# Unused expert tiles moved into a branch, with p7's additions, the last bias and the squared sums rearranged, in a two-layer fp32 kernel

## The chip, the cores and the metric

The kernel runs on one core of a Trainium2 chip. The metric is the device time of one execution in microseconds. A core has five engines that run beside each other, each in the order of its own instruction stream: TensorE (PE in the profile; PEld is its weight load), VectorE (DVE), ScalarE (ACT), GpSimd (POOL) and SyncE (SP, which here issues DMAs). They wait for each other through semaphores.

## What is computed

The input is 2048 tokens of 512 numbers. The first layer adds three things to them: a gated linear attention of 32 heads of 128, a shared expert, and a mixture of 16 small experts of which each token takes two. A second, smaller layer follows (attention of one head and a low-rank mixture). All of it is fp32. Cut to the part that the change is about:

```python
logits = xt @ router_w + router_b
scores = softmax(logits) + router_bias
keep   = the 2 best of 4 groups of experts, by each group's best score
idx    = the 2 best experts among the kept           # for each of 2048 tokens
for e in range(16):
    h = silu(xt @ ew1[e] + eb1[e]) * (xt @ ew2[e] + eb2[e])
    y += gate[:, e] * (h @ ew3[e] + eb3[e])
y += shared expert, with its own last bias sb3

attn = causal linear attention with decay, heads of 128
out  = (sigmoid(x @ gate_w.T) * norm_w * attn * rsqrt(mean(attn**2) + eps)) @ out_w.T
```

## The kernel before

**Opening** (to about 120 us). Tokens are normalized, transposed and routed. Each token's two choices become slots of a list that is sorted by expert; each expert's part of the list is rounded up to whole tiles of 128 slots. The worst routing needs `NMT` = 47 tiles, so the kernel has 47. `ends` holds, in its last column, the number of tiles that the routing really uses; `whose` says whose token stands in a slot, `own_` and `rows_` which expert owns a tile. A tile that no expert uses is worked on as if it were the last expert's, and nobody reads its rows of `yd`.

**Attention.** The long middle part is 4 chunks of 512 tokens (i) by 8 groups of four heads (g): 32 *units*, numbered i * 8 + g. The projection of a unit is a product of matrices cut into halves, done with 7 half-size products instead of 8, two levels deep: 7 *outer products* p1, p2, p6, p5, p3, p7, p4 (`ORDER`), each of 7 inner products of four 128 x 128 matmuls (`product`, L730 to L738; L735 is the matmul). In the first chunk some outer products are done plainly. `Outer.result` (L1106) takes an inner sum out of PSUM: into r and from there into a (POOL, DVE) or straight into b, c or d. Four quarters a, b, c, d of the unit's result become whole after p2, p3, p7 and p4, and each then goes through `Quarter` (L825): silu and gate on ACT, scores, attention, squared sums, and the output projection (`Unit.project`, L944), which sums over all units of a chunk in `acc`. When a chunk's last unit is done, `done`, `combine` and `finish` (L1030, L634, L640) turn `acc` into the attention's part of the layer's result.

**The order of the work** is written out by hand. After each inner product `slot()` (L755) is called; `later(n, f)` puts a piece of other work n slots ahead, and `slot()` runs at most one or two of those that are due, where some named pieces don't count. On ACT and POOL the instructions keep the order of the source (`manual_schedule`); on TensorE, DVE and SP a scheduler may move them. DVE's order in the built program is thus not always that of the source.

**Expert tiles** run inside the units of chunks 1 to 3. `expert(j)` (L1187) starts tile j; `Expert` (L765) gathers its 128 tokens and the expert's weights by two indirect DMAs on POOL (L772, L777), turns the tokens with 4 transposes (L786), gathers the bias (L792), multiplies (8 matmuls, L804; one of 512 columns, L816) and stores 256 KB to `yd` (L822). On TensorE an fp32 matmul is two instructions, a transpose is one. From the unit where g is 0 of each chunk, two tiles are started, else three in early units (`EARLY`) and two later:

```python
for e in range(3 if g > 0 and i * NG + g < FROM + EARLY else 2):
    if todo:
        later((24 if g == 0 else 1) + 16 * e, partial(expert, todo.pop(0)))
```

**Buffers.** r and the tiles' result ye share three buffers of the tag "sum" (2 KB a partition each). The last bias of the shared expert, `sb3`, takes one of them at each chunk's end: `load_sum` (L1023) loads it, and `last_bias` (L651) adds it at once with four additions on POOL. Weights w rotate in three buffers, the output projection's weights wo in seven. `attend` (L864) squares 512 columns on ACT and adds all 512 to `sums` on POOL; at a chunk's end the two halves are added. Of `p7` the result r is added into a on POOL and into c on DVE, in the same step.

## Time and profile before

| what | us |
|---|---|
| median of 3 runs | 2780.84 (2780.56 to 2783.33) |
| the profiled execution's own time | 2780.53 |
| its span, first to last instruction | 2778.5 |
| granted TensorE clock, mean | 0.997 of full |
| TensorE busy / weight loads | 2733.5 / 2522.7 |
| DVE / ACT / POOL busy | 1627.6 / 947.2 / 1649.8 |

Names in the profile are those of the program without buffer numbers: `ps_a`, `ps_b`, `ps_e`, `ps_sc`, `ps_o` are PSUM banks, `xt` the tokens' sums, `w` the weights. L100 is the line of a helper that adds or subtracts (L101 in the changed kernel), so additions are told apart by their tiles, not by their line; `c<-c,r` may add into a, b, c or d, which all bear the name c. In a row of a stretch, "busy (x)" is busy time and number of instructions. A bracket at the end of a timeline's line is the engine's idle time just before it and what ended it. Matmuls overlap each other, so the durations of single matmuls don't add up to time; distances between starts do.

The chunks show in the profile: the first (units 0 to 7) runs to about 701, the second to 1305, the third to 1896, the fourth to 2464, and the second layer fills the rest.

### The profile page before, as it was taken

The numbers are of one execution on the slowest core, as the hardware profiler recorded it, in microseconds if no ns is written. First come the engines' busy times: TensorE is split into PE (matmuls) and PEld (weight loads), VectorE is DVE, ScalarE is ACT, GpSimd is POOL, SyncE is SP. The second block draws the span as 40 slices with busy tenths as digits, with TensorE's granted clock in tenths as the row PEclk, the third lists the DMA queues.
The fourth block names the chain that finished last, engine by engine and source line by source line (L and its number), as shares of the span: only waits on it lengthen the run. The fifth ranks groups of instructions, "written<-read, shape, count | busy, mean of one in ns | idle before, by whom it ended". The sixth has DMA issues, their size and how long they took to land.

```text
span 2778.5 us, 49222 instructions
## 1 busy us (share of the span) xinstructions
PE 2733.5 (98%) x19492; PEld 2522.7 (91%) x19492; DVE 1627.6 (59%) x2733; ACT 947.2 (34%) x1683; POOL 1649.8 (59%) x1422
## 2 busy tenths in 40 slices
PE   9999999999999999999999999999999999999999
PEld 5699999999999999999999999999999999987877
DVE  7656777776545555555545555555555555667663
ACT  5232222222433333333343333334433333432221
POOL 6477777776566666665855555556555567553210
PEclk9999999999999999999999999999999999999999
DMA  7898898888977777777877777787877788653211
GB/s 296 310 339 335 311 334 325 337 315 330 352 274 261 288 272 277 265 280 288 304 250 253 253 257 251 264 288 268 281 255 255 270 298 295 218 215 124 78 63 63
DMA packets 155445, 735.87 MB, mean 265 GB/s; under 512 B 18768, under 2 KB 25296, under 8 KB 112848
## 3 DMA queue, kind: packets, MB, share of 16 engines
q1 hardware_dynamic: 137056, 661.89, 64.8%
q0 software_dynamic: 17872, 70.32, 7.7%
q8 instruction: 154, 2.52, 0.4%
q14 instruction: 75, 0.61, 0.1%
q10 hardware_dynamic: 288, 0.52, 0.1%
HBM read 587.84 MB, written 144.04 MB: 263 GB/s over the span
## 4 chain that ended last, share of the span: by engine, by line
PE 86%; DVE 6%; POOL 3%; issue 3%; DMA 2%; ACT 0%; SPq 0%; DVEq 0%; POOLq 0%; ACTq 0%
PE ps_a L735 25%; PE ps_e L735 13%; PE ps_sc L948 10%; PE ps_b L735 7%; PE ps_sc L968 4%; PE ps_o L869 4%; PE ps_sc L857 3%; PE ps_sc L804 3%; PE ps_o L870 2%; PE ps_sc L858 2%; PE ps_a L1676 2%; PE ps_sc L816 1%; DVE w L100 1%; PE ps_a L1579 1%; PE ps_a L359 1%
## 5 line engine op out<-in xcount | busy, mean ns | idle before, releaser
L735 PE MATMUL ps_a<-xt,w 128*128 128x128 f32 x5376 | 751.3, 276 | 16.3 <-DVE r L100 7.6
L735 PEld LDWEIGHTS ps_a<-xt,w 128*128 128x128 f32 x5376 | 686.7, 192 | 46.0 <-issue 14.1
L100 POOL TENSOR_TENSOR c<-c 128x512 f32<-128x512 f32 x240 | 305.2, 1286 | 265.7 <-DVE c L100 263.1
L1103 ACT COPY cp<-ps_a 128x512 f32<-128x512 f32 x384 | 224.0, 584 | 659.9 <-PE ps_a L735 636.9
L100 POOL TENSOR_TENSOR c<-c,r 128x512 f32<-128x512 f32 x264 | 345.8, 1332 | 167.1 <-DVE r L100 166.6
L735 PE MATMUL ps_e<-xt,w 128*128 128x128 f32 x2688 | 374.5, 275 | 0.6 <-DVE r L100 0.3
L735 PEld LDWEIGHTS ps_e<-xt,w 128*128 128x128 f32 x2688 | 341.4, 192 | 6.7 <-issue 2.9
L735 PE MATMUL ps_a<-w,xt 128*128 128x128 f32 x1792 | 346.8, 275 | 0.0
L100 POOL TENSOR_TENSOR w<-w 128x512 f32<-128x512 f32 x224 | 297.7, 1337 | 80.5 <-DVE w L100 32.9
L100 POOL TENSOR_TENSOR sums<-sums,sq 128x512 f32<-128x512 f32 x120 | 155.8, 1298 | 277.4 <-ACT sq L884 276.8
L948 PE MATMUL ps_sc<-wo,gT 128*128 128x256 f32 x1288 | 304.9, 380 | 2.8 <-POOL gT L100 2.8
L735 PEld LDWEIGHTS ps_a<-w,xt 128*128 128x128 f32 x1792 | 272.4, 192 | 0.0
L948 PEld LDWEIGHTS ps_sc<-wo,gT 128*128 128x128 f32 x1288 | 232.9, 190 | 30.9 <-POOL gT L100 3.1
L100 DVE TENSOR_TENSOR acc<-ps_sc,acc 128x512 f32<-128x512 f32 x208 | 142.7, 689 | 195.2 <-PE ps_sc L948 150.6
L891 DVE SCALAR_TENSOR_TENSOR gT<-ps_o,nw,c 128x256 f32<-128x256 f32 x256 | 112.0, 479 | 216.1 <-ACT sq L884 206.0
L735 PE MATMUL ps_b<-xt,w 128*128 128x128 f32 x1536 | 214.8, 276 | 6.5 <-issue 3.7
L100 DVE TENSOR_TENSOR c<-ps_a,c 128x512 f32<-128x512 f32 x216 | 146.8, 687 | 120.7 <-PE ps_a L735 115.4
L735 PEld LDWEIGHTS ps_b<-xt,w 128*128 128x128 f32 x1536 | 195.1, 193 | 9.0 <-issue 5.7
L832 ACT ACTIVATE c<-c 128x512 f32<-128x512 f32 x256 | 150.3, 628 | 146.0 <-DVE c L100 127.9
L884 ACT ACTIVATE sq<-ps_o 128x512 f32<-128x512 f32 x120 | 71.7, 597 | 358.1 <-PE ps_o L870 352.7
L100 DVE TENSOR_TENSOR s<-ps_sc,decay 128x384 f32<-128x384 f32 x256 | 139.7, 553 | 79.9 <-PE ps_sc L858 77.2
L735 PE MATMUL ps_e<-w,xt 128*128 128x128 f32 x896 | 173.5, 275 | 0.0
(297 smaller groups left out, 4723.3 us busy)
## 6 DMA issues: line engine op xcount, KB each, us to landing
w<-in_w_att_dram SPq DMA_DIRECT2D x56, 1024.0 KB
w<-in_w_att_dram SPq DMA_DIRECT2D x72, 768.0 KB
st<-in_w_att_dram SPq DMA_DIRECT2D x32, 1024.0 KB
wo<-in_w_out_dram SPq DMA_DIRECT2D x113, 256.0 KB
decay<-dec SPq DMA_DIRECT2D x64, 384.0 KB
w<-ws0p SPq DMA_DIRECT2D x12, 1792.0 KB
w<-ws1p SPq DMA_DIRECT2D x12, 1792.0 KB
w<-ws2p SPq DMA_DIRECT2D x12, 1792.0 KB
```

What stands on the lines that cost most here:

```text
L100: (eng or nc.vector).tensor_tensor(o, a, b, op)
L735: mm(bank[:, bass.ts(ty, P)], a, b, start=(first and ty == 0), stop=True, skip_group_check=True,)
L804: mm(pu[:, bass.ts(n, P)], w12[:, n, c, :], self.xeT[:, c, :], start=(c == 0), stop=(c == NC - 1),)
L832: nc.scalar.activation(qk, qk, AF.Silu)
L857: mm(p[:, 0:S], self.c[:, 2 * hh, P : 2 * P], q, start=True, stop=True)
L858: mm(p[:, S : S + P], self.c[:, 2 * hh + 1, P : 2 * P], q[:, 1, :], start=True, stop=True,)
L869: mm(po[:, bass.ts(hh, S)], v[:, 0, :], self.s[:, hh, 0:S], start=True, stop=False)
L884: nc.scalar.activation(sq, po, AF.Square)
L891: nc.vector.scalar_tensor_tensor(gT[:, h, :].rearrange("p (t n) -> p t n", t=2), po[:, bass.ts(h, S)].rearrange("p (t n) -> p t n", t=2), ...
L948: mm(py[:, bass.ts(t, S)], self.O[p][:, hh, bass.ts(t, P)], self.wo[p][:, hh, :], start=(t == 0 and hh == 0), stop=(hh == 1), skip_group_c ...
L968: mm(py[:, bass.ts(h, S)], gT[:, hh, bass.ts(t, P)], self.wo[pair, h][:, hh, :], start=(h == 0 and hh == 0), stop=(hh == 1), skip_group_ch ...
L1103: nc.scalar.copy(c, bank)
```

## The change

Five things are changed together; the diff follows.

1. **A branch.** Only tiles 0 to 35 (`USUAL`) are run in the units. The other 11 stand, one behind the other, in `beyond()`, under a condition on the number of used tiles, which the opening copies into `used`. It is called once, before p2 of unit 27 (the unit where i is 3 and g is 3). Tiles are started as three each in units 9 to 12 and two each in units 13 to 15, 17 to 23, 25 and 26, and none where g is 0. The rows of `yd` that a passed-by tile would have written are filled with a copy of tokens by 11 DMAs from DRAM to DRAM, one a unit (units 8 to 18).
2. **p7's additions.** r is now added into c on POOL, at once, and into a on DVE; the additions into a are collected and written out after the third result, and again after the fourth.
3. **The last bias** is loaded into a buffer of the tag "wo", and its four additions on POOL become pieces of their own, 10, 13, 16 and 19 slots later; the load comes 1 slot after the quarter becomes whole instead of 5.
4. **Squared sums.** `sums` holds 256 columns instead of 512; the two halves of a square are added to it one after the other, and the addition at the chunk's end goes.
5. **Buffers and times.** r and ye get four buffers instead of three, and the second part of the slots' table is read 10 slots earlier (`take_table` at 30 for 40).

```diff
@@ -38,6 +38,7 @@
 
 NMT = (NT * TOP + E * (P - 1)) // P
 NSLOT = NMT * P
+USUAL = 36
 READ = 32
 WROW = 2 * NC * INTER + C + 2
 K, TOPK, RANK, SCALING = 64, 16, 16, 2.0
@@ -549,6 +550,8 @@
     own = disp.tile([P, NMT], FP, name="own")
     nc.vector.tensor_reduce(own, owner, AX.X, ALU.add)
     nc.vector.tensor_scalar(own_, own, float(E - 1), None, ALU.min)
+    used = const.tile([P, 1], I32, name="used")
+    nc.vector.tensor_copy(used, ends[:, 0, E - 1 : E])
     nc.vector.tensor_scalar(own, own, float(E - 1), float(P), ALU.min, ALU.mult)
     nc.vector.tensor_scalar(rows_, own, part, None, ALU.add)
 
@@ -759,7 +762,7 @@
             while pieces and pieces[0][0] <= now[0] and n < (2 if len(pieces) > 12 else 1):
                 f = pieces.pop(0)[2]
                 f()
-                n += getattr(f, "func", f).__name__ not in ("silu", "bias", "gate", "read_table", "take_table", "scatter", "load_sum", "sums1", "sums2", "sums3", "sums4", "settle0", "settle1", "out_sum", "combine", "finish", "store")
+                n += getattr(f, "func", f).__name__ not in ("bias_sum", "silu", "bias", "gate", "fill_tile", "read_table", "take_table", "scatter", "load_sum", "sums1", "sums2", "sums3", "sums4", "settle0", "settle1", "out_sum", "combine", "finish", "store")
 
 
         class Expert:
@@ -817,7 +820,7 @@
                     py, self.he, self.we[:, 2 * NC * INTER : 2 * NC * INTER + C],
                     start=True, stop=True,
                 )
-                ye = attn.tile([P, C], FP, tag="sum", name="ye", bufs=3)
+                ye = attn.tile([P, C], FP, tag="sum", name="ye", bufs=4)
                 add(ye, py, self.xe)
                 nc.sync.dma_start(out=yd[bass.ts(self.j, P), :], in_=ye)
 
@@ -840,7 +843,7 @@
 
             def begin(self):
                 if self.u.g == NG - 1 and (self.pair, self.b) == (1, 0):
-                    later(5, self.u.load_sum)
+                    later(1, self.u.load_sum)
                 later(2, partial(self.silu, 0))
                 later(3, partial(self.silu, 1))
                 later(4, self.gate)
@@ -875,16 +878,15 @@
                     return
                 u = self.u
                 if u.i not in sums_:
-                    sums_[u.i] = attn.tile([P, 2, CH], FP, tag="sums", name="sums")
+                    sums_[u.i] = attn.tile([P, 2, S], FP, tag="sums", name="sums")
                 sums = sums_[u.i][:, self.b, :]
+                sq = attn.tile([P, CH], FP, tag="sq" if u.i else "cp", name="sq", bufs=1 if u.i else 5)
+                nc.scalar.activation(sq, po, AF.Square)
                 if u.g == 0 and self.pair == 0:
-                    nc.scalar.activation(sums, po, AF.Square)
+                    add(sums, sq[:, 0:S], sq[:, S:], nc.gpsimd)
                 else:
-                    sq = attn.tile([P, CH], FP, tag="sq" if u.i else "cp", name="sq", bufs=1 if u.i else 5)
-                    nc.scalar.activation(sq, po, AF.Square)
-                    add(sums, sums, sq, nc.gpsimd)
-                if u.g == NG - 1 and self.pair == 1:
-                    add(sums[:, 0:S], sums[:, 0:S], sums[:, S:], nc.gpsimd)
+                    for h in range(2):
+                        add(sums, sums, sq[:, bass.ts(h, S)], nc.gpsimd)
                 gT = u.gated()
                 for h in range(2):
                     n = u.g * HG + self.pair * 2 + h
@@ -1025,7 +1027,14 @@
                 if self.i + 1 < NCH:
                     self.r = spare8()
                     nc.sync.dma_start(out=self.r, in_=xr[self.i])
-                    last_bias(self.r, attn.tile([P, C], FP, tag="sum", name="sb3", bufs=3))
+                    b3_t = attn.tile([P, C], FP, tag="wo", name="sb3", bufs=7)
+                    nc.sync.dma_start(out=b3_t, in_=b3[E : E + 1].to_broadcast([P, C]))
+
+                    def bias_sum(t):
+                        add(self.r[:, t, :], self.r[:, t, :], b3_t, nc.gpsimd)
+
+                    for t in range(TPC):
+                        later(10 + 3 * t, partial(bias_sum, t))
 
             def done(self):
                 if self.g < NG - 1:
@@ -1066,7 +1075,7 @@
 
             def __init__(self, unit, p):
                 self.u, self.p = unit, p
-                self.steps = []
+                self.steps, self.added = [], []
                 self.following = None
                 self.w = weights(unit.i, unit.g, p, self.steps)
                 if unit.g == 0:
@@ -1127,15 +1136,21 @@
                         c_ = u.tile("c")[:, q]
                         add(c_, bank, c_)
                 else:
-                    r = attn.tile([P, 512], FP, tag="sum", name="r", bufs=3)
+                    r = attn.tile([P, 512], FP, tag="sum", name="r", bufs=4)
                     if c is None:
                         nc.scalar.copy(r, bank)
                     else:
                         add(r, bank, c)
-                    add(a, a, r, pool)
-                    if p == "p7":
+                    if p != "p7":
+                        add(a, a, r, pool)
+                    else:
                         c_ = u.tile("c")[:, q]
-                        add(c_, c_, r)
+                        add(c_, c_, r, pool)
+
+                        self.added.append(partial(add, a, a, r))
+                        if (i, j) in ((1, 1), (0, 1)):
+                            while self.added:
+                                self.added.pop(0)()
                 whole = dict(p2=("b", 0, 0), p3=("d", 0, 1), p7=("c", 1, 1), p4=("a", 1, 0)).get(p)
                 if whole and (i, j) == (0, 1):
                     Quarter(u, whole[1], whole[2], u.tile(whole[0])).begin()
@@ -1173,8 +1188,8 @@
                 self.result(0, 1, self.a, None)
 
         FROM = NG
-        EARLY = 8
-        todo = list(range(NMT))
+        EARLY = 5
+        todo = list(range(USUAL))
         plan = [(i, g, p) for i in range(NCH) for g in range(NG) for p in ORDER]
         units = []
 
@@ -1190,6 +1205,21 @@
             later(12, e.bias)
             later(14, e.up)
             later(19, e.down)
+
+        def fill_tile(j):
+
+            nc.sync.dma_start(out=yd[bass.ts(j, P), :], in_=x[0:P, :])
+
+        def beyond():
+
+            n_used = nc.values_load(used[0:1, 0:1], min_val=0, max_val=NMT)
+            with tc.If(n_used > USUAL):
+                for j in range(USUAL, NMT):
+                    e = Expert(j)
+                    e.turn()
+                    e.bias()
+                    e.up()
+                    e.down()
 
         def scatter(t, n):
 
@@ -1221,7 +1251,7 @@
                 if n == 0:
                     read_table(1)
 
-            later(40, take_table)
+            later(30, take_table)
 
         def low_sums(n):
 
@@ -1325,9 +1355,11 @@
             if k == 0:
                 u.load_decay()
                 if i * NG + g >= FROM:
-                    for e in range(3 if g > 0 and i * NG + g < FROM + EARLY else 2):
+                    for e in range(0 if g == 0 else 3 if i * NG + g < FROM + EARLY else 2):
                         if todo:
-                            later((24 if g == 0 else 1) + 16 * e, partial(expert, todo.pop(0)))
+                            later(1 + 16 * e, partial(expert, todo.pop(0)))
+                if FROM <= i * NG + g < FROM + NMT - USUAL:
+                    later(30, partial(fill_tile, USUAL + i * NG + g - FROM))
                 if i == 0:
                     for e in range(max(5 * g - 3, 0), 5 * g + 2 if g < NG - 1 else 0):
                         later(10 * (e - 5 * g) + 35, partial(scatter, e // TOP, e % TOP))
@@ -1339,6 +1371,9 @@
                     wrapped_up()
             if k == 2:
                 u.load_decay()
+            if (i, g, k) == (NCH - 1, NG - 5, 1):
+                assert not todo
+                beyond()
             u.load_out(k)
             last = outers[n - 1] if n and sevenfold(n - 1) else None
             if not sevenfold(n):
```

## The prediction, written before the result was known

> **What bounds the kernel now.** I read the page's busy rows and its chain first. (Times in us unless marked; "tile" is one expert tile of 128 slots, "unit" one group of four heads of one 512-token chunk.)

> ```profile
> PE 2733.5 (98%) x19492; PEld 2522.7 (91%) x19492; DVE 1627.6 (59%) x2733; ACT 947.2 (34%) x1683; POOL 1649.8 (59%) x1422
> PE 86%; DVE 6%; POOL 3%; issue 3%; DMA 2%; ACT 0%; SPq 0%; DVEq 0%; POOLq 0%; ACTq 0%
> ```

> TensorE is busy nearly all the time and holds 86% of the chain that ended last: what leaves TensorE's stream shortens the run, what leaves DVE or POOL does so only where TensorE waits for it. So I looked next for what one tile costs TensorE. The table of stretches gives it: three stretches, each exactly one unit long (from a mark to the same mark a unit later), with three tiles, two tiles and none.

> ```profile
> core 0: us, PE busy (x) PEld busy (x) DVE busy (x) ACT busy (x) POOL busy (x), PEclk, DMA share, GB/s
> 1077.20:1152.99 75.79, 75.79 (x580) 71.96 (x579) 40.86 (x62) 27.51 (x52) 49.45 (x41) 1.00 0.75 271
> 1449.20:1522.38 73.18, 72.77 (x557) 69.36 (x557) 39.81 (x60) 27.48 (x50) 40.80 (x34) 1.00 0.72 255
> 2183.91:2250.93 67.02, 66.61 (x513) 64.15 (x513) 36.07 (x54) 26.55 (x48) 43.76 (x32) 1.00 0.74 261
> ```

> The second and third differ by 44 matmuls, two tiles of 22 (4 transposes, 16 halves of the up products, 2 of the down product), and by 6.16: a tile costs 3.08 of wall time. Three tiles cost 75.79 - 67.02 = 8.77, as the third fills a wait of 0.4 that the other two units show (busy 0.41 under the span). Last I read TensorE's own waits, the only other time to be won (columns: total, times, longest):

> ```profile
> PE ps_a L735 <- DVE r L100: 7.6, 16, 1.3
> PE ps_a L735 <- ACT cp L1103: 5.2, 3, 1.8
> PE ps_sc L948 <- POOL gT L100: 2.8, 2, 1.6
> ```

> **Tiles.** 47 run now, whatever the routing. Counting the reference's routing of its own inputs, five experts get 1859, 140, 46, 3 and 2048 choices: 15 + 2 + 1 + 1 + 16 = 35 used tiles, under 36, so the branch is passed by and 11 tiles of TensorE work go. With f(1) = 3.08, f(2) = 6.16, f(3) = 8.77 a unit: units 8 to 27 hold now 2 units with one tile, 9 with two, 9 with three (140.5); then 12 with two and 4 with three (109.0). **-31.5**; by 11 x 3.08 it would be -33.9, my lower end. What else a tile costs, three indirect DMAs on POOL (1.03, 1.00 and 1.07 each) and work on ACT and DVE, lies beside TensorE.

> **Fourth buffer for r and ye.** Three of the 16 waits for DVE r (1.32 at 773.68, 0.49 at 1381.59, 0.48 at 1969.95) stand in the first p4 after a chunk change, where the eviction waited for POOL to release one of three buffers. A fourth removes that: **-2.3** (0 if POOL is then late anyway).

> **p7's additions.** The remaining 13 waits are this pattern, on DVE in the unit at 2250:

> ```profile
> 2247.08 0.69 DVE L100 TENSOR_TENSOR r<-ps_e,cp 128x512 f32<-128x512 f32 x1 [1.19 <-PE ps_e L735]
> 2247.88 1.80 DVE L100 TENSOR_TENSOR c<-c,r 128x512 f32<-128x512 f32 x1
> 2249.60 0.68 DVE L100 TENSOR_TENSOR r<-ps_b,cp 128x512 f32<-128x512 f32 x1
> 2250.20 0.68 DVE L100 TENSOR_TENSOR r<-ps_a,cp 128x512 f32<-128x512 f32 x1
> ```

> A 1.80 addition stands between the first eviction and the two that free PSUM, and p3 of the same product waits 0.41 for the last. The diff defers that addition in the source until after the third eviction. But DVE's order is the scheduler's, and in the built program the row after the first r is again an addition of r (now into a), then two r, then the rest: the order of before, 4 additions on DVE and 4 on POOL as before, sharing time as before. I take **0**. Bounds: -9.9 (0.58 from when p3's first matmul was due, 2250.35, to its start at 2250.93, in the 17 units that will have two tiles or none and no chunk change) if the wait does go; no loss, since a was last written by POOL two outer products earlier.

> **Bias by pieces.** At a chunk's end POOL now sits in front of a load:

> ```profile
> 1322.60 4.96 POOL L100 TENSOR_TENSOR spare<-spare,sb 128x512 f32<-128x512 f32 x4 [11.43 <-DMA sb<-in_b_dram]
> ```

> Behind it are queued sums and gT, and TensorE waits 1.65 (1330.87) and 1.10 (2335.51) for gT. Ten slots later the load has landed, and the additions come one by one: **-2.8** (0 if a single 1.33 addition still meets gT). The bias now rotates in wo's seven buffers; SP is in order, so a later wo load could slip; the longest such wait today is 11.1, and loads lie 1.5 outer products ahead: 0.

> **Chunk changes.** Two ACT cp waits (1.67 and 1.68) follow from ACT standing behind a copy into acc that waits for DVE to finish the old chunk. Without tiles in the first unit POOL loses three DMA issues (3.1) ahead of that finish. Between 0 and -3.4 I take half: **-1.7**.

> **Squares.** Two additions of 256 columns for one of 512:

> ```profile
> L100 POOL TENSOR_TENSOR sums<-sums,sq 128x512 f32<-128x512 f32 x120 | 155.8, 1298 | 277.4 <-ACT sq L884 276.8
> L100 POOL TENSOR_TENSOR sums<-sums 128x256 f32<-128x256 f32 x8 | 5.8, 726 | 0.6
> ```

> 2 x 0.726 - 1.298 = 0.15 a quarter, 24 in all with the eight first squares (8 x 1.45) and without the eight last sums: POOL's, who loses 34 with the tiles. 0; were POOL's gT on the path each time, 92 x 0.15 = +14. The 11 fills of unused rows, one copy of 256 KB each, replace tile transfers of over 1.5 MB each in the queue: 0 (one landing, 6.7, if one load were held up). The copy of the count in the opening is one small DVE instruction (nearest row 0.16): 0.

> **The branch.** New, once, in unit 27. Every engine reads the count, compares and jumps; TensorE passes over some 500 instructions, then waits for its own last matmul; SP waits for all its loads, POOL for its gathers. Behind TensorE's instruction everything is queued. No row shows a jump. The nearest is an engine's instructions arriving by DMA, and an awaited small DMA from issue to landing (those that fill or read xw):

> ```profile
> q8 instruction: 154, 2.52, 0.4%
> ```

> ```profile
> DMA to landing us min/median/max: 3.4/6.7/12.3
> ```

> 154 packets of 16 KB, 0.4% x 16 x 2778.5 / 154 = 1.15 each: TensorE's code comes in pages, and 500 instructions of its 39,000 (2 x 19492) are two of them. Bounds: 0.3 (a matmul's own end) and two landings of 12.3, 24.6; not below, as the branch removes nothing. I take one median landing, **+6.7**. SP's stop is hidden: in a ring of three a load of weights is issued about 1.5 outer products (1.5 x 67.02 / 7 = 14) before its use.

> [...] The granted clock is 1.00 in all three stretches, and no wait of TensorE in the trace is over 2.6. [...]

> **Sum**: -31.5 - 2.3 - 0 - 2.8 - 1.7 + 6.7 = -31.6. From the profiled execution's own 2780.53 (span 2778.5 and 2.0 around it; the median of the runs is 2780.84): **2749**.

> **Rivals.**
> - *The addition moves and the branch is cheap.* For: the same addition takes 0.68 where POOL is quiet (at 2391.55), so if POOL's into c starts later than its addition into a does now, the 1.80 shrinks and r is free in time. Against: the built order, and POOL starts on the same r. 2749 - 9.9 - 3.3 (a landing of 3.4) = 2736.
> - *The branch empties all engines*: two landings, 24.6, as in and out of the jump both miss; against: the exit lies next to the code it enters. 2749 + 17.9 = 2767.
> - *The branch is not passed by* (slower). Place: unit 27, price: 11 tiles in series, TensorE idle between. One tile's chain by rows: two gathers 2.03, landing 6.7, transposes 0.60, copy 0.68, up 1.95, silu 0.37, product 0.35, down 1.02, sum 0.69 = 14.4; 158 for 11, 79 if two buffers hide half. 2749 + 79 to 158 = 2828 to 2907. It decides from the 37th used tile on; my count is 35.
> - *Nothing gained*: a branch of over 33 eats all, 2775 to 2786; no row is that long.

> **How the numbers follow.** Forecast, 2741 to 2757: 0.62 (branch 3.4 to 12.3, the small waits gone or not). First rival, 2731 to 2741: 0.16. Second, 2757 to 2775: 0.15. Not passed by: 0.04. Nothing gained: 0.03. About 0.2% (5.6) can be told from no change. Faster 0.62 + 0.16 + 0.15 = 0.93, within 0.03, slower 0.04. 2733 to 2764 holds all of the forecast, most of the first rival and over half of the second: 0.84.

> **What would show it.** Units with equal tiles still 67.02 and 73.18; 36 down products (72 halves); one gap on TensorE in unit 27 of 3 to 12; no POOL wait for the bias load; p7's wait of 0.41 still there. I am wrong if units change by more than 0.6, if the gap is over 12.3, or if down products number 94.

## The result, and the profile after

The changed kernel takes 2757.95 us (median of 4 runs, 2754.57 to 2759.92) against 2780.70 for the kernel before beside it: a ratio of 0.9910, with a 95% interval of 0.9899 to 0.9922. It is faster by 22.8, where 31.6 was forecast. The profiled execution took 2759.92, with a span of 2758.2 (before: 2780.53 and 2778.5), at a mean granted clock of 0.994 (before 0.997).

The page of the changed kernel begins with the busy rows:

```profile
PE 2704.0 (98%) x19250; PEld 2499.6 (91%) x19250; DVE 1597.3 (58%) x2701; ACT 943.9 (34%) x1672; POOL 1652.5 (60%) x1509
```

TensorE has 242 matmuls fewer, 11 tiles of 22: the branch is passed by. POOL has 87 instructions more and is as busy as before, though it lost the gathers of 11 tiles. Next the table of stretches, again one unit each: two tiles, no tile, and the unit of the branch (columns as in the table shown before).

```profile
1438.30:1510.80 72.50, 72.50 (x558) 69.32 (x557) 38.85 (x60) 27.32 (x50) 42.03 (x38) 1.00 0.71 257
2161.85:2228.75 66.90, 66.45 (x514) 64.03 (x512) 35.57 (x54) 27.06 (x48) 43.90 (x36) 1.00 0.71 254
2089.80:2161.85 72.05, 68.29 (x515) 65.35 (x514) 35.45 (x54) 26.62 (x47) 35.87 (x32) 0.98 0.68 238
```

In the first row the span and TensorE's busy time are the same, 72.50: the wait of 0.41 is gone, and the unit is 0.68 shorter than the 73.18 of before. The third row is the branch's unit: TensorE is busy 3.76 less than the span, and the clock is 0.98 of full. TensorE's waits tell the other side:

```profile
PE ps_a L738 <- ACT cp L1112: 11.8, 6, 2.6
PE ps_o L872 <- DVE s L101: 6.2, 6, 2.6
...
PE ps_sc L950 <- PEq L1216: 3.8, 1, 3.8
...
PE ps_sc L950 <- POOL gT L101: 1.4, 1, 1.4
...
PE ps_a L738 <- DVE r L101: 0.4, 1, 0.4
```

The 16 waits for DVE's r (7.6) are gone but for one of 0.4. In their place the waits for ACT's cp went from 5.2 to 11.8, those for DVE's s from 1.3 to 6.2, and the branch (L1216) added one of 3.8.

**Where the time went.** I cut the profiled execution, from its first matmul to its last, at the first matmul of every unit and took from each unit's length what its matmuls take at the mean spacing in a unit of the changed kernel in which nothing is waited for (unit 19: 0.1115 a matmul of 128 columns, 0.2164 of 256, 0.4305 of 512; a tile 3.09; other widths, in the opening and the second layer, at their means there). What is left over is waiting and half clock (stretches in which the granted clock was 0.5), here called loss.

| part | before | after | change |
|---|---|---|---|
| undisturbed matmuls | | | -34.0 |
| loss in units 17 to 23, 25, 26 | 7.6 | 0.0 | -7.6 |
| loss in units 9 to 13 and 28 to 31 | 6.6 | 4.2 | -2.4 |
| loss in units 14 and 15 | 0.4 | 4.1 | +3.7 |
| loss in unit 8 | 0.2 | 5.0 | +4.8 |
| loss in units 16 and 24 (first of a chunk) | 6.1 | 9.5 | +3.5 |
| loss in unit 27 (branch) | 0.7 | 5.7 | +5.0 |
| loss before unit 8 | 34.4 | 38.1 | +3.7 |
| loss in the second layer | 12.3 | 14.5 | +2.2 |
| sum | | | -21.1 |

So the work fell by somewhat more than forecast, p7's wait went against the forecast, and the six rows with a plus gave 23 back.

### The profile page after: what moved, and what is told of

It reads as the page before. It is cut to its first block, busy times and chain, and to the rows that moved or that the text cites. A ratio compares the mean times of both kernels' runs of the same rounds, so it can differ in the third digit from the quotient of the medians.

```text
span 2758.2 us, 48688 instructions
## 1 busy us (share of the span) xinstructions
PE 2704.0 (98%) x19250; PEld 2499.6 (91%) x19250; DVE 1597.3 (58%) x2701; ACT 943.9 (34%) x1672; POOL 1652.5 (60%) x1509
## 3 DMA queue, kind: packets, MB, share of 16 engines
q8 instruction: 154, 2.52, 0.4%
## 5 line engine op out<-in xcount | busy, mean ns | idle before, releaser
L738 PE MATMUL ps_a<-xt,w 128*128 128x128 f32 x5376 | 752.1, 277 | 16.6 <-ACT cp L1112 11.8
L101 POOL TENSOR_TENSOR c<-c,r 128x512 f32<-128x512 f32 x264 | 362.4, 1396 | 161.2 <-DVE r L101 157.7
L101 POOL TENSOR_TENSOR sums<-sums,sq 128x256 f32<-128x256 f32 x240 | 180.3, 751 | 307.7 <-ACT sq L884 297.9
L950 PE MATMUL ps_sc<-wo,gT 128*128 128x256 f32 x1288 | 306.9, 382 | 5.2 <-PEq L1216 3.8
L950 PEld LDWEIGHTS ps_sc<-wo,gT 128*128 128x128 f32 x1288 | 233.9, 192 | 31.6 <-issue 4.4
L884 ACT ACTIVATE sq<-ps_o 128x512 f32<-128x512 f32 x128 | 76.5, 597 | 380.2 <-PE ps_o L873 371.8
```

What stands on the lines that cost most here:

```text
L101: (eng or nc.vector).tensor_tensor(o, a, b, op)
L738: mm(bank[:, bass.ts(ty, P)], a, b, start=(first and ty == 0), stop=True, skip_group_check=True,)
L884: nc.scalar.activation(sq, po, AF.Square)
L950: mm(py[:, bass.ts(t, S)], self.O[p][:, hh, bass.ts(t, P)], self.wo[p][:, hh, :], start=(t == 0 and hh == 0), stop=(hh == 1), skip_group_c ...
```

## The experiments

Theories. **A**: p7's wait went because the exchange of engines makes POOL start its addition after DVE's, not before it. Rivals: the fourth buffer took the wait away, or the additions written later did. **B**: the branch costs what TensorE waits for the code behind the jump, and a stretch of half clock. Rival: reading the count and jumping cost it. **C**: the new waits come from the exchange, as c is now made whole by POOL. Rivals: from the tiles' new places, the squares, or the bias. All kernels were run in sets of four beside the kernel before on the same chip (its medians 2782.56, 2781.94 and 2782.60).

| run | median us | ratio to before, 95% interval |
|---|---|---|
| changed kernel | 2757.95 | 0.9910 (0.9899 to 0.9922) |
| m2_after_again | 2756.02 | 0.9902 (0.9885 to 0.9918) |
| e1_no_branch | 2748.29 | 0.9881 (0.9867 to 0.9895) |
| e2_p7_as_before | 2765.91 | 0.9943 (0.9931 to 0.9954) |
| e5_p7_defer_only | 2762.84 | 0.9927 (0.9914 to 0.9940) |
| e4_p7_pool_later | 2762.19 | 0.9926 (0.9914 to 0.9938) |
| h1_tiles_alone | 2754.52 | 0.9899 (0.9883 to 0.9914) |
| f2_squares_whole | 2753.53 | 0.9903 (0.9887 to 0.9918) |
| f3_bias_whole | 2757.70 | 0.9904 (0.9888 to 0.9920) |
| g3_both | 2756.17 | 0.9912 (0.9898 to 0.9926) |
| m1_short_branch | 2751.15 | 0.9882 (0.9866 to 0.9899) |
| k1_first_and_deferred | 2751.76 | 0.9891 (0.9875 to 0.9908) |
| k2_tile_in_first_units | 2746.95 | 0.9873 (0.9856 to 0.9889) |

Many of these differ by less than their intervals, so I read them by the lengths of units in their profiles. These agree to 0.02 between executions in the steady units (18, 28), and all kernels here but k2 and the kernel before place the tiles alike:

| unit | 8 | 14 | 15 | 16 | 18 | 24 | 27 | 28 |
|---|---|---|---|---|---|---|---|---|
| changed | 71.41 | 74.54 | 75.19 | 71.91 | 72.50 | 71.77 | 72.03 | 67.05 |
| m2, again | 71.41 | 74.56 | 75.20 | 73.17 | 72.50 | 71.79 | 72.18 | 67.05 |
| e1, no branch | 68.66 | 76.30 | 75.20 | 72.03 | 72.50 | 71.79 | 66.34 | 66.34 |
| e2, p7 as before | 73.78 | 73.18 | 73.83 | 72.12 | 73.18 | 72.60 | 73.90 | 66.99 |
| e5, later only | 72.53 | 73.31 | 73.84 | 71.79 | 73.18 | 71.78 | 73.78 | 66.99 |
| e4, POOL later | 71.41 | 73.17 | 73.83 | 72.12 | 73.18 | 72.59 | 71.97 | 66.98 |
| h1, tiles alone | 72.33 | 73.18 | 73.83 | 72.13 | 73.17 | 71.44 | 67.01 | 67.01 |
| f2, squares | 71.43 | 74.50 | 75.19 | 71.25 | 72.50 | 69.86 | 72.04 | 66.34 |
| f3, bias | 71.36 | 74.53 | 75.20 | 73.16 | 72.50 | 71.78 | 72.00 | 66.34 |
| g3 | 68.66 | 73.29 | 73.97 | 74.01 | 72.50 | 83.50 | 66.34 | 66.34 |
| m1, short branch | 71.43 | 74.53 | 75.19 | 73.17 | 72.50 | 71.77 | 67.42 | 66.34 |
| k1 | 71.44 | 73.30 | 73.94 | 72.38 | 72.50 | 71.79 | 72.10 | 66.34 |

### p7: as before, and with the engines exchanged back

e2 writes p7's additions as before:

```diff
-                    if p != "p7":
-                        add(a, a, r, pool)
-                    else:
-                        c_ = u.tile("c")[:, q]
-                        add(c_, c_, r, pool)
-                        self.added.append(partial(add, a, a, r))
...
+                    add(a, a, r, pool)
+                    if p == "p7":
+                        c_ = u.tile("c")[:, q]
+                        add(c_, c_, r)
```

> The changed kernel with p7's additions written as before: r into a on POOL and into c on DVE, at once; all else as changed, four buffers for r and ye too. Theory (who starts first): on DVE's side the order is RARRAAA in both; the wait of p3 for r went because POOL's addition, now into c, starts after DVE's instead of 30 ns ahead, so DVE's takes 0.69 instead of 1.8. Then the waits PE ps_a <- DVE r return (13 or more, 0.41 each), units with two tiles are at 73.18 again instead of 72.50, about +10; and c is whole earlier, so the waits of 1.77 at 1156 and 1231 and the 2.6 at 767 go, about -6 to -8: 2758 to 2763 in sum. Rival (the fourth buffer took the wait away): units stay at 72.50 and the new waits go, 2750 to 2752.

e5 keeps the collecting and exchanges only the engines:

```diff
-                        add(c_, c_, r, pool)
-                        self.added.append(partial(add, a, a, r))
+                        add(a, a, r, pool)
+                        self.added.append(partial(add, c_, c_, r))
```

> The changed kernel with the additions of p7 collected and written out later as in the change, but with the engines of before: a on POOL, c on DVE (collected). The orders of DVE and of POOL, by tile names, are line for line those of the changed kernel; only which of a and c an addition writes is exchanged. Theory (the engines' exchange decides who starts first): the waits PE ps_a <- DVE r return, 73.18 in the steady units with two tiles, and the new waits behind POOL's c go: 2758 to 2763, as with the additions as before. Rival (writing them later took the wait away): 72.50, and about 2750 to 2752.

Measured: 2765.91 and 2762.84, and 73.18 in the steady units of both: the wait is back, with four buffers and with the additions written later. Theory A stands and both its rivals fall. (e2's time lies 2.9 above its forecast: the wait of 2.6 in unit 8 stayed, and unit 8 got one of 0.9 for r besides.) The rows show how. In the changed kernel, DVE and then POOL in a steady unit (start, duration):

```profile
1869.73 0.69 DVE L101 TENSOR_TENSOR r<-ps_e,cp 128x512 f32<-128x512 f32 x1 [1.13 <-PE ps_e L738]
1870.52 0.69 DVE L101 TENSOR_TENSOR c<-c,r 128x512 f32<-128x512 f32 x1
1871.13 0.69 DVE L101 TENSOR_TENSOR r<-ps_b,cp 128x512 f32<-128x512 f32 x1
```

```profile
1870.56 3.01 POOL L101 TENSOR_TENSOR c<-c,r 128x512 f32<-128x512 f32 x2 [5.62 <-DVE r L101]
```

And in e5, the same unit, DVE, POOL and the matmul of p3:

```profile
1871.33 1.80 DVE L101 TENSOR_TENSOR c<-c,r 128x512 f32<-128x512 f32 x1
1873.05 0.68 DVE L101 TENSOR_TENSOR r<-ps_b,cp 128x512 f32<-128x512 f32 x1
```

```profile
1871.31 1.28 POOL L101 TENSOR_TENSOR c<-c,r 128x512 f32<-128x512 f32 x1 [5.55 <-DVE r L101]
```

```profile
1874.38 0.94 PE L738 MATMUL ps_a<-xt,w 128*128 128x128 f32 x6 [0.41 <-DVE r L101]
```

The order on DVE is the same, r, addition, r. But in e5 POOL starts 0.02 ahead and DVE's addition takes 1.80; in the changed kernel DVE starts 0.04 ahead and takes 0.69, and it is POOL's first addition that takes 1.79 instead of 1.28 (the row joins two). At this pair, in all of these kernels, whoever starts first is undisturbed, and the other ends 1.8 after that start, in both orders. A shift of 65 ns decides over 1.1 on DVE. In the built program POOL's addition into c waits for one thing more than that into a, an earlier addition into the same c by POOL itself; that this makes the 65 ns was not tested by itself.

The delay falls on one of the two alone: in e5 DVE's addition, 0.69 when it starts first, ends 0.55 after POOL's of 1.28, and in the changed kernel POOL's ends 1.14 after DVE's of 0.69. What holds the second one back, these rows don't show. The forecast let both "share" the time and did not ask who starts first.

Theory C falls in part: units 14 and 15 drop to 73.18 and 73.83 in e2 and e5, so the waits of 1.77 there are the exchange's (as is one of 1.1 early in unit 16, which e2 and e5 have not), but unit 8 keeps its wait of 2.6 for DVE's s. In unit 14 of the changed kernel, ACT shows why:

```profile
1152.72 1.15 ACT L835 ACTIVATE c<-c 128x512 f32<-128x512 f32 x2 [5.01 <-POOL c L101]
```

POOL's additions into c stand behind sums of wo in its queue; ACT waits 5.01 for c, its copies come late, and TensorE waits for them.

e4 leaves c on DVE and means to hold POOL's addition into a back by writing it later:

```diff
-                        add(c_, c_, r, pool)
-                        self.added.append(partial(add, a, a, r))
+                        add(c_, c_, r)
+                        self.added.append(partial(add, a, a, r, pool))
```

> The changed kernel with c on DVE at once, and a on POOL collected and written out after the third and the fourth result. Theory (who starts first): DVE's first addition has the path to itself, takes about 0.7, and p3 does not wait; c is whole as early as before. So units stay at 72.50 without the waits at 767, 1156 and 1231: 2757.95 less 5 to 8, 2750 to 2753. Rival A: r is held until POOL's late addition, and DVE waits for a buffer of r: 2758 or more. Rival B: POOL's late addition then meets DVE's third one, which p4 or its quarter waits for: 2755 to 2765.

Measured: 2762.19 and 73.18, neither the theory nor its rivals. POOL started 0.02 or more ahead of DVE in all units but the first with this pattern: its queue held nothing else at that point, so the addition that was written later started as early as before. Writing it later gave POOL nothing to wait for.

### The branch

e1 drops the call (`beyond()`).

> The changed kernel without the call that reads the count and branches; the 11 tiles behind the branch are left out (this routing uses 35, so nothing that is read is missing). Theory: the branch costs the gap on TensorE in unit 27 (PE ps_sc L950 <- PEq L1216, 3.8) and the half-clock stretch of 3.413 behind it (eight matmuls at twice their time, about 1.9), together 5.7: 2757.95 - 5.7 = 2752.2, unit 27 at 66.34 as unit 29. Rival A: only the gap goes and a later wait takes its place: under 3, 2755 or more. Rival B: the stop of SP (2100.1 to 2109.1) also holds back loads and costs more than the gap: over 8, under 2750.

Unit 27 is at 66.34 as expected, 5.69 less; unit 28 loses 0.7, where POOL had started first after the branch. Units 29 and 30 are as long as in the changed kernel (66.34 and 68.44), so no load that SP's stop held back shows, though the time, 2748.29, lies where that rival (B) had it. It fell by 9.7, not 6.4: unit 8 was 2.75 shorter, the part before it 3.4, and unit 14 1.8 longer, though nothing is changed there. m2 ran the changed kernel once more to see whether such parts belong to the kernel.

> The changed kernel itself once more, beside the others of this set. The excess of the first eight units (3.9 over the kernel before) and of unit 8 differs among the variants though their code is the same there. Theory: that part is not from the change but differs from one profiled execution to the next, by where the half-clock stretches fall: the first eight units vary by 1 to 4, units 9 to 31 agree with the first profile within 0.3 but for units 14 to 16, where a stretch may or may not start. Rival: it is the change's own: the first eight units and unit 8 come out the same within 0.5. The time: 2755 to 2760.

The loss before unit 8 was 35.2 instead of 38.1, and unit 16 was 1.26 longer; unit 8 was the same. Over all profiles of variants the loss before unit 8 is 33.0 to 38.1 and that of the second layer 12.8 to 14.8: differences of single executions, and two of the table's rows (+3.7, +2.2) are not shown to be the change's.

The traces say what made unit 8 shorter in e1. Near its end one pair of additions starts almost at once, POOL's and DVE's; here in the changed kernel and then in e1:

```profile
762.75 1.27 POOL L101 TENSOR_TENSOR wo<-wo 128x512 f32<-128x512 f32 x1
762.76 3.47 DVE L101 TENSOR_TENSOR c<-c,r 128x512 f32<-128x512 f32 x2
```

```profile
759.30 1.82 POOL L101 TENSOR_TENSOR wo<-wo 128x512 f32<-128x512 f32 x1
759.31 2.36 DVE L101 TENSOR_TENSOR c<-c,r 128x512 f32<-128x512 f32 x2
```

In six profiles (the changed kernel, m2, f2, f3, m1, k1) POOL starts 11 to 26 ns ahead and is the undisturbed one; in e1 and g3 it starts 12 and 11 ahead and DVE is, so that DVE's scores s come 1.1 sooner, TensorE's wait is 1.45 instead of 2.56, and no half clock follows. At a distance of some 12 ns the recorded starts don't tell who goes first.

m1 puts one tile behind the branch instead of 11:

```diff
-                for j in range(USUAL, NMT):
+                for j in range(USUAL, USUAL + 1):
```

> The changed kernel with only one tile behind the branch instead of 11 (tiles 37 to 46 are left out; this routing uses 35). TensorE then jumps over about 44 matmul and load instructions instead of some 500. Theory: the gap of 3.8 is mostly the fetch of the code behind the jump, which is not yet there when 500 instructions are passed over; with 44 the code is there and the gap falls under 1, without a half-clock stretch behind it: unit 27 at 66.5 to 67.5 instead of 72.03, 2753. Rival: the gap is the reading of the count, the compare and the jump themselves, or the stop for TensorE's last matmuls, and stays at 3 to 4: unit 27 at 71 to 72, 2758.

Measured: unit 27 at 67.42, 2751.15 (4.9 less than m2 beside it). That unit is still 1.1 longer than in e1, and 0.4 of this is p7's wait, which is back in it. The branch instruction of TensorE's sequencer in the changed kernel, with another engine's (duration in ns):

```profile
L1216 PEldq COMPARE_BRANCH  x1: 5007/5007/5007, 2103.9 to 2103.9; - x1
...
L1216 DVEq COMPARE_BRANCH  x1: 72/72/72, 2105.3 to 2105.3; - x1
```

and in m1:

```profile
L1216 PEldq COMPARE_BRANCH  x1: 236/236/236, 2102.1 to 2102.1; - x1
```

5007 over 11 tiles, 236 over one: reading the count and jumping are cheap, and theory B stands. (The other engines took 45 to 72 for it in both kernels.) The DMA packets of the changed kernel's trace show the fetch itself: while the branch lasts, from 2103.93 to 2108.94, two packets of 16 KB move in the queue for instructions, q8 (2104.76 to 2105.82 and 2105.45 to 2107.48), where those around them come 12.4 to 22.0 apart; in m1 the next one starts at 2102.44, after the branch. The next matmuls in the changed kernel, eight, took 3.63 at half clock, and in m1 1.89:

```profile
2109.25 3.63 PE L950 MATMUL ps_sc<-wo,gT 128*128 128x256 f32 x8 [3.76 <-PEq L1216]
```

```profile
2104.54 1.89 PE L950 MATMUL ps_sc<-wo,gT 128*128 128x256 f32 x8
```

### Tiles, squares and bias one by one

h1 is the kernel before with the new number and places of the tiles and the fills, and nothing else:

```diff
-        EARLY = 8
-        todo = list(range(NMT))
+        EARLY = 5
+        todo = list(range(USUAL))
...
-                    for e in range(3 if g > 0 and i * NG + g < FROM + EARLY else 2):
+                    for e in range(0 if g == 0 else 3 if i * NG + g < FROM + EARLY else 2):
```

> The kernel before with the tiles' part alone: 36 tiles on the new schedule, the 11 fills, and no branch (tiles beyond 36 are left out; this routing uses 35). Theory: TensorE's work falls by 11 x 3.1 = 34.1 and p7's wait of 0.41 stays in the steady units (73.18), 2780.8 - 34.1 = 2747, less the two of the 16 waits for a buffer of r that stand behind a first unit's tiles; no waits of 1.77 at units 14 and 15, since c stays on DVE. At the chunk changes the ACT cp wait grows from 1.7 by up to 0.6, because TensorE has no tile's transposes to do in the first unit of a chunk. In all 2744 to 2749. Rival: the new schedule itself makes the waits at 767, 1156 and 1231: 2751 to 2757.

Measured: 2754.52, outside the theory's 2744 to 2749. Units 14 and 15 have no wait of 1.77, so those are not the schedule's; but unit 8 has its wait of 2.6 and its half clock (loss 5.9 against 0.2 before), and units 16 and 24 lost 9.4 together against 6.1; of this, 0.75 and 1.70 are waits for DVE's r behind p7's additions. The wait for gT at 1330 and those for a buffer of r (1.3 in unit 9, 0.5 in 17 and 25) are gone already here, with three buffers and the bias at once: what the forecast gave to the fourth buffer and to the bias, the tiles' going brought.

f3 puts the bias back as it was, with four buffers:

```diff
...
-                    b3_t = attn.tile([P, C], FP, tag="wo", name="sb3", bufs=7)
...
-                        later(10 + 3 * t, partial(bias_sum, t))
+                    last_bias(self.r, attn.tile([P, C], FP, tag="sum", name="sb3", bufs=4))
```

> The changed kernel with the last bias as before: loaded 5 slots after the quarter, added at once by four additions on POOL, in a buffer shared with r and ye (four). Theory: the wait of POOL for this load (11.4) returns and with it TensorE's wait for gT at the ends of chunks 2 and 3 (1.65 and 1.1 before, about 1.4 in the changed kernel at 2313 only): +1 to +3, 2759 to 2761. Rival: the pieces of the bias are what makes the finish of a chunk late; then the ACT cp waits at 1360 and 1938 fall by 1 each and the half-clock stretch goes: 2754 to 2757.

Measured: 2757.70, no difference, and no wait for gT at 1330, though POOL waits for the load again, for 7.4 where it was 11.4:

```profile
1316.13 4.97 POOL L101 TENSOR_TENSOR spare<-spare,sb 128x512 f32<-128x512 f32 x4 [7.37 <-DMA sb<-in_b_dram]
```

Both the theory's +1 to +3 and the rival fall: the waits for ACT's cp in units 16 and 24 fell from 2.65 to 2.10, but waits of 0.3 for DVE's c came beside them, and the units are as long as in m2. The bias by pieces is worth nothing that these runs tell.

f2 sums the squares as before, and for the space has three buffers for r and ye:

```diff
-                    sums_[u.i] = attn.tile([P, 2, S], FP, tag="sums", name="sums")
+                    sums_[u.i] = attn.tile([P, 2, CH], FP, tag="sums", name="sums")
...
-                    add(sums, sq[:, 0:S], sq[:, S:], nc.gpsimd)
+                    nc.scalar.activation(sums, po, AF.Square)
...
```

> The changed kernel with the squares summed as before (512 columns, the first square of a chunk straight from ACT) and, for the space, three buffers for r and ye. Theory: at a chunk change POOL no longer has the 1.18 of the first squares' sum in front of the last addition of the old chunk's acc, so DVE's finish and the ACT copy behind it come about 0.6 to 1.2 sooner, and the ACT cp wait at 1360 and 1938 falls from 2.65 and 2.81 to about 1.7; the half-clock stretch of 3.413 at 1938.7 goes too (about 1.7). POOL is 24 busier or less by 24 elsewhere without effect. The fourth buffer's price shows as waits for r in units 9, 17 and 25 (1.3, 0.5, 0.5). In sum 2757.95 - 2 to 4 + 2 = 2756 to 2758. Rival: the squares have nothing to do with it and the wait stays at 2.6; then 2760.

Measured: 2753.53, below the theory's 2756 to 2758. The ACT cp waits in units 16 and 24 are 1.98 instead of 2.65, as the theory has it. Unit 24 is 1.9 shorter: 0.7 of this is the wait, and the other 1.2 is the stretch of half clock that followed the longer wait and did not come here. POOL at that place in the changed kernel:

```profile
1928.36 2.50 POOL L101 TENSOR_TENSOR acc<-acc 128x512 f32<-128x512 f32 x2
1930.81 1.18 POOL L101 TENSOR_TENSOR sums<-sq 128x256 f32<-128x256 f32 x1
1931.95 1.72 POOL L101 TENSOR_TENSOR acc<-acc 128x512 f32<-128x512 f32 x1
```

and in f2:

```profile
1925.22 4.19 POOL L101 TENSOR_TENSOR acc<-acc 128x512 f32<-128x512 f32 x3
```

The first squares' sum of the new chunk now stands ahead of the last addition of the old chunk, for which DVE's finish, then ACT's copy into acc, then TensorE wait. The waits for r that I expected in units 9, 17 and 25 did not show; unit 21 had one of 0.77 (in h1 too), in which DVE's r waits for POOL to release a buffer, and that is what the fourth buffer takes away. Units 19, 20, 22, 23, 25 and 26 were 0.23 longer; whether by the buffers or by the squares, these runs don't tell.

### Candidates

g3 exchanges the engines for the first of p7's four results only, so that POOL still starts second but c is whole early, and moves the branch to unit 24, where TensorE waits anyway:

```diff
+                    elif (i, j) == (1, 0):
+                        add(c_, c_, r, pool)
+                        add(a, a, r)
+                    else:
+                        add(a, a, r, pool)
+                        add(c_, c_, r)
...
-            if (i, g, k) == (NCH - 1, NG - 5, 1):
+            if (i, g, k) == (NCH - 1, 0, 5):
```

> A candidate for a faster version. The changed kernel with two edits: of p7 only the first result has its engines exchanged (c on POOL, a on DVE), the other three have a on POOL and c on DVE; and the branch is called in unit 24 ahead of p7, where TensorE waits 2.8 for ACT anyway, instead of in unit 27. Theory: the first result's exchange alone makes POOL start after DVE, so the steady units stay at 72.50 and 66.34; c is whole early, so the waits at 1156 and 1231 (1.77 each) and 1305 (1.28) go, about 4.8; unit 27 falls by 5.7 and unit 24 keeps one gap of about 4 with its half-clock stretch, 3.9 - 2.8 = 1.1 more than now; 2757.95 - 4.8 - 5.7 + 1.1 = 2748 to 2750. Rival: in unit 24 the gap of the branch and the wait for ACT add up instead of covering each other: 2751 to 2754. Rival: POOL's start goes by the later results, and the units are at 73.18 again: 10 more, 2758.

Measured: 2756.17, worse than the theory and than its first rival. The exchange of one result does what it should (72.50, and 73.29 and 73.97 in units 14 and 15; unit 16 got a wait of 1.45 for DVE, which k1, with the additions collected, has not). The branch does not: unit 24 grew by 11.7. ACT's queue after it:

```profile
1930.71 0.59 ACT L958 COPY acc<-ps_sc 128x512 f32<-128x512 f32 x1 [9.70 <-DVE spare L649]
1939.78 1.28 ACT L1112 ACT_TABLE_LOAD   x1 [8.49 <-PEq L1215]
```

ACT is 9.70 late from the chunk's finish, then idles 8.49, which the profile puts down to TensorE's sequencer at the branch, then loads a table, and TensorE's next inner product waits 5.0 for its copy: the two delays stand one after the other.

k1 takes the exchange of one result, keeps DVE's additions collected, and leaves the branch in unit 27:

```diff
-                        add(c_, c_, r, pool)
-                        self.added.append(partial(add, a, a, r))
+                        x_, y_ = (c_, a) if (i, j) == (1, 0) else (a, c_)
+                        add(x_, x_, r, pool)
+                        self.added.append(partial(add, y_, y_, r))
```

> A candidate. The changed kernel with p7's engines exchanged for the first of the four results only (c on POOL, a on DVE), the others as before (a on POOL, c on DVE), and DVE's additions collected and written out later as in the change; the branch stays in unit 27. Theory: POOL starts after DVE in every steady unit (72.50 and 66.34), c is whole early, and units 14 and 15 lose their waits of 1.77, as in the candidate with the moved branch (73.3 and 74.0 instead of 74.5 and 75.2); units 16 and 24 stay at 71.8, since DVE's order is RRRAAA there again. 2757.95 less 2.5 to 5: 2753 to 2756. Rival: units 16 or 24 get a wait for DVE of 1.7 as there, and nothing is left.

k2 is k1 with one tile in each chunk's first unit again (and one fewer in units 11, 12 and 26):

```diff
-                    for e in range(0 if g == 0 else 3 if i * NG + g < FROM + EARLY else 2):
+                    for e in range(1 if g == 0 else 3 if i * NG + g < FROM + EARLY else 2):
...
-        EARLY = 5
+        EARLY = 3
```

> The candidate before this one with one tile in each chunk's first unit again (units 8, 16 and 24, started at slot 24), three tiles in units 9 and 10 only, two in 11 to 15, 17 to 23 and 25, one in 26; 36 in all. Theory: the tiles of the first units gave TensorE work while ACT and DVE were behind, and their going, not the other edits, made the waits of 2.6 to 2.8 there (unit 8 at 767, unit 16 at 1360, unit 24 at 1938) and the half-clock stretches behind them. With one tile each, the excess of unit 8 falls from 6.1 to under 3, those of 16 and 24 from 6.2 and 6.1 to 3.5 to 5; in sum 4 to 8 less than the candidate: 2746 to 2751. Rival: POOL's three DMA issues ahead of the old chunk's finish give the gain back: same within 2.

Measured: 2751.76 and 2746.95, with m2 at 2756.02 beside them: k2 is the fastest version that holds all the work, a ratio of 0.9873 to the kernel before. k1's time lies below its forecast of 2753 to 2756, k2's inside its own. In k1 units 14 and 15 are 1.25 shorter each, and 16 and 24 keep their waits. In k2 the loss of unit 8 falls from 5.0 to 0.6 and that of units 16 and 24 from 10.0 to 6.0, what it was before the change: a tile there is not only work, it is also cover. Its matmuls stand between those that wait for DVE and ACT, in TensorE's fixed order. In the changed kernel TensorE waits 2.56 for DVE's s in unit 8 and 2.65 for ACT's cp in units 16 and 24 each, in k1 the same within 0.03; in k2 the first wait is gone and the other two are 2.33 and 2.35. So in unit 8 the whole wait went, and in units 16 and 24 only 0.3 each. The rest of the 4.0 there is mostly half clock, which k1 has in both units and k2 in neither; that the tile keeps it away is shown by this one profile of each only. Of the gain, 2.5 came back as new waits in units 9, 12 and 13.

## Why the prediction was right and wrong

The time, 2757.95, lies in the range of 2733 to 2764 and 0.95 above the forecast's own case (2741 to 2757), at the edge of the "two landings" case, but not for that case's reason: the branch was cheaper than its forecast. The sum (2749) missed by 9 through steps that went both ways, so that the time lies in the range is in part luck: e2, in which p7's wait stays as the forecast had it, takes 2765.91, outside. By one of the prediction's own signs ("if units change by more than 0.6") it was wrong, as units with equal tiles changed by 0.68. In runs, the tiles alone brought 27.4 (h1), the other edits without the branch 6.2 more (e1), and the branch took 7.7 (m2) to 9.7 back.

- **Tiles, -31.5**: right for TensorE's work, too much for the time. 242 matmuls less are -34.0; the third tile of a unit costs 3.5 (75.97 against 72.50), not 2.6, mostly since the wait that it filled is gone. But "what else a tile costs lies beside TensorE" looked at one side only: what a tile gives, cover for the chunk's first units, was not asked. h1 and k2 show it: 4.5 to 5.8 in unit 8 (only 2.1 in e1 and g3, where its wait was 1.45 and the clock stayed whole), and 3 to 4 in units 16 and 24, part of it half clock.
- **p7's additions, 0**: this step failed. The order was read rightly from the built program, and "sharing time as before" was wrong: POOL starts 65 ns later against DVE, DVE's addition takes 0.69 instead of 1.80, and the wait of 0.41 goes (e2, e5). The bound (-9.9) and the first rival's reason ("if POOL's into c starts later") were right. Units 17 to 23, 25, 26 and 29 gained about 0.7 each; the price for c on POOL, 2.5 in units 14 and 15 (k1) and 1.1 in unit 16, was not foreseen.
- **Fourth buffer, -2.3, and bias, -2.8**: the three waits for a buffer and the wait for gT of 1.65 are gone, but through the tiles (h1), not through these edits; the second wait for gT, 1.10, stayed, at 1.4. The fourth buffer saves 0.8 in unit 21, the bias nothing (f3).
- **Chunk changes, -1.7**: the wrong sign. The ACT cp waits grew from 1.7 to 2.65, by 0.67 through the squares' sum on POOL (f2) and 0.3 through the missing tile (k2, h1).
- **Squares, 0 on TensorE**: right for the 24 on POOL, wrong for the one addition at each chunk change that stands on the path: 0.67 of wait in units 16 and 24 each, and in unit 24 a stretch of half clock behind it (1.2).
- **Branch, +6.7**: 5.7 (unit 27 in e1), of 3.8 wait and 1.9 behind it, nearly all half clock; the fetch was the right mechanism (m1), and the half clock, which the sum left out, is a third of it. That the size came so near is luck: the wait alone was little over half of the forecast. In other profiles with this branch unit 27 is 5.0 (e4) to 6.9 (e2) longer than a unit without tiles, as one or two stretches of half clock follow.

## What to carry to other kernels

Where DVE and POOL add at the same time, look at which of them starts first, to the hundredth of a microsecond: here 65 ns decided whether DVE's addition took 0.69 or 1.80, and a wait of 0.41 on TensorE came or went while the order of rows on each engine stayed the same. Work that is taken out of a full engine was also cover for whatever is late at that place, so before removing it see what stands behind it in each place, and leave a piece where a late engine needs it. A branch over unrolled code can cost TensorE the fetch of what it jumps to (a wait of 3.8 here over 11 tiles, 0.15 over one in m1), and in g3 it didn't hide in another wait, as the late engine had to take the branch too.

## What the runs showed of the hardware that was not expected

```profile
764.53:767.94 3.41, 1.09 (x6) 1.05 (x7) 2.64 (x4) 0.00 (x0) 3.41 (x3) 1.00 0.23 89
767.94:771.35 3.41, 3.41 (x18) 3.33 (x17) 0.00 (x0) 0.58 (x1) 1.91 (x2) 0.50 0.37 139
1358.44:1361.85 3.41, 1.55 (x13) 1.55 (x14) 1.23 (x2) 1.86 (x4) 1.76 (x2) 1.00 0.62 231
1361.85:1365.26 3.41, 3.41 (x33) 3.41 (x32) 2.79 (x5) 3.38 (x6) 1.96 (x2) 1.00 0.96 288
```

and then e1 in unit 14, where a wait of 1.9 was enough:

```profile
1147.23:1150.64 3.41, 1.53 (x12) 1.29 (x11) 0.69 (x1) 3.38 (x7) 3.41 (x4) 1.00 0.96 231
1150.64:1154.05 3.41, 3.41 (x14) 3.10 (x13) 1.43 (x3) 2.47 (x6) 2.96 (x3) 0.50 0.88 349
```

Here, then, a wait that left TensorE busy 1.54 or less in one stretch of the grid cost 1.26 and 1.76 on top (half a stretch of 3.413, 1.7, is my estimate), and a wait of 2.65 that lay across a line of the grid cost nothing more. Where the grid falls differs from one execution to the next: one line is at 1358.44 in the changed kernel and at 1357.80 in m2. So the changed kernel kept its clock behind the wait of 2.65 in unit 16, m2 lost it there (73.17 instead of 71.91), and e1 lost it in unit 14 (76.30 instead of 74.54) and kept it in unit 8, after a wait of 1.45.
